# One more key tile in parts in two half groups, more sums by transfer, and spreads on ScalarE: a fused attention and local-attention kernel

## The chip, the cores and the metric

The kernel runs on one core of a Trainium2 chip. The metric is the device time of one execution, in microseconds (us). Five engines work side by side, each through its own list of instructions in order: TensorE (PE, matrix products; its weight loads are shown apart as PEld), VectorE (DVE), ScalarE (ACT), GpSimd (POOL) and SyncE (SP, which here only starts transfers). They wait for one another by semaphores. Transfers are started from SP, ACT or POOL and run on 16 DMA engines.

## What is computed

The input is x, of shape (4, 64, 64, 256): four pictures of 4096 pixels with 256 channels. Two layers follow each other. Cut to what matters:

```python
# layer 0: attention of every pixel over all 4096 of its picture
q, k, v = x @ Wq + bq, x @ Wk + bk, x @ Wv + bv        # q, k: 32 channels, v: 256
attn = softmax(einsum('bnd,bmd->bnm', q, k))
x = gamma * einsum('bnm,bmc->bnc', attn, v) + x

# layer 1: a 3x3 perception, two pointwise products, then attention over a 3x3 neighbourhood
perceived = depthwise_conv3x3(x, w_perc)               # 768 channels
hid = gelu(w_up1 @ perceived)                          # 512 channels
h = x + w_up2 @ hid                                    # 256 channels
out = h + local_attention_3x3(h, w_qkv)
```

Everything is in 32-bit floats. All biases are there, too.

## The kernel before

**Slots.** The work goes through 32 slots, 8 for each picture; a slot is a block of 512 query pixels of layer 0. While slot s does the big attention of its block, layer 1 follows behind in the same slot's instructions: the perception of block s-2, the hidden products of block s-3 and the local attention of block s-5. Everything is written out by hand in program order, and no planner moves it: what an engine does next is what the program says next for that engine.

**Points.** A slot has 16 points. At each, one half group of 256 keys (two key tiles of 128) is worked on; I number half groups n = 0 to 15. At point n the loop (L1246 on) does, in this order:

- loads on SP: for odd half groups with a tile in parts, the parts of the values of half group n+1 (load_one, "vo"); at even points the keys and values of groups ahead
- on ScalarE, the high part of the weights of half group n+1 where that is wanted (high_part, "ph", for both tiles; high_one, "oh", for one)
- energy: q times k for half group n+2 on TensorE ("e"), and the exponential of it on ScalarE ("p", three buffers)
- send: the transfer of p of half group n+1 where its denominators are summed by transfer
- the jobs of layer 1 for this point (hidden_part, local_product, update, guide, local_values, scores, local_sum, border)
- product: weights times values for half group n on TensorE, into four "acc" banks
- add_up on VectorE for half group n+1: low and gap parts ("pl", "pg", or "ol", "og" for one tile), and the sum of the denominators "den"
- so many steps of the convolution on VectorE (perceive, L666 and L672) as the list `share` gives for this point

After point 15 come partial_sums (den is transposed and reduced, twice with the local sums; "turned", "parts") and finish: a small product on TensorE that adds over partitions (dps, L551), its reciprocal on VectorE, the spread of the reciprocals to 512 columns (on_all, L538: a copy that repeats each, then a transpose), and the output of layer 0 with it (L561 on ScalarE, L567, L569, L575 on VectorE). Then the next slot's first energy and jobs.

**In parts.** A product of full 32-bit numbers takes TensorE several passes. To save passes, a weight p is cut into a high part (on ScalarE: p times 1 - 2^-13, rounded to the shorter form float32r), a low part p - high, and a "gap" high - 4096 low (both on VectorE); the values v have been cut in the same way beforehand (project_v, L334; kept in DRAM as packed_h, packed_f, packed_o). Three products of short numbers then stand for one of long ones, the gap's into acc banks of its own, and finish puts them together. Half groups 2, 4, ..., 14 have both tiles in parts (IN_PARTS), half groups 3, 5, ..., 13 the second tile alone (ONE_IN_PARTS); the first tile of these, and half groups 0, 1 and 15, go through TensorE whole. One-tile parts are made only in "full" slots: 3 to 30 without 7, 15 and 23. Slots 1, 2, 7, 15 and 23 are not full (7, 15 and 23 also project the keys and values of the next picture), nor are 0 and 31.

**Buffers.** vo, oh, ol and og share the four buffers of the tag "vs", in turn. ph, pl and pg have one buffer each. sent tiles (below) take the tag "sent" (one buffer) for odd half groups and "xc" (two buffers) for even ones; "turned" and the staged inputs also live in "xc".

**Denominators.** den must be the sum of p over all 16 half groups. VectorE adds most of it (L504). In full slots half groups 3 to 13 are instead added up by transfers that POOL starts (send, L470: the first of a parity copies p to the sent tile (L476), the others accumulate there (L478)), one chain for odd and one for even half groups; VectorE adds the two sent tiles to den at the end (L513).

Of the kernel before, what the change touches and what calls it, by code (L numbers as in the profile page):

```python
# [52 lines left out]
ONE_IN_PARTS = (3, 5, 7, 9, 11, 13)  # L53
BY_DMA = (ONE_IN_PARTS, (4, 6, 8, 10, 12))

# [5 lines left out]
def attention_then_perception_kernel(  # L61
# [37 lines left out]
    def unshifted():  # L99
# [107 lines left out]
        queries, keys, values, forms, staged = {}, {}, {}, {}, {}  # L207
# [7 lines left out]
        packed_o = tc.dram_tile([P, NSLOT, 2, C], F32, name="packed_o")  # L215
# [10 lines left out]
        def one_in_parts(s, n):  # L226
            return full(s) and n in ONE_IN_PARTS

# [69 lines left out]
        def block(s, G):  # L298
            return s - s % NBLK + G
# [24 lines left out]
        def load_one(s, n):  # L324
            forms[s, n] = tile_of([P, NB], "vs", f"vo_{s}_{n}", 4)
            nc.sync.dma_start(
                out=forms[s, n].rearrange("p (f c) -> p f c", c=C),
                in_=packed_o[:, block(s, n // 2)],
            )
# [4 lines left out]
        def project_v(s, pair, tag="m"):  # L334
            xc = staged[s]
            ps = bank(tag, f"v_{s}_{pair}")
            for i in range(2):
                for kin in range(CH):
                    nc.tensor.matmul(  # L339
                        ps[:, i * C : (i + 1) * C],  # L340
                        lhsT=xc[:, kin, bass.ts(2 * pair + i, P)], rhs=wv[:, kin, :],
                        start=(kin == 0), stop=(kin == CH - 1),
                    )
            of = ps.rearrange("p (t c) -> p t c", c=C)
            n = 2 * (s % NBLK) + pair
            split, one = n in IN_PARTS, n in ONE_IN_PARTS
            h = packed_h[:, s, bass.ts(pair, 2 * C)].rearrange("p (t c) -> p t c", c=C)
            if not split or s < NBLK or s >= NSLOT - NBLK:
                if s >= NBLK:
                    v = fresh(f"vs_{s}_{pair}")  # L350
                else:
                    if (0, s) not in values:
                        values[0, s] = tile_of([P, TPB, C], ("v", "vf")[s % 2], f"v_0_{s}", 2)
                    v = values[0, s][:, 2 * pair : 2 * pair + 2, :]
                nc.scalar.activation(v, of, AF.Identity, scale=SPLIT / (SPLIT + 1.0))  # L355
                nc.scalar.dma_start(
                    out=packed_v[:, bass.ts(2 * s + pair, 2 * C)],
                    in_=v.rearrange("p t c -> p (t c)"),
                )
                if not split:  # L360
                    tiles = slice(0, 1 if one else 2)
                    nc.gpsimd.dma_start(out=h[:, tiles], in_=v[:, tiles])
            if split:
                high = fresh(f"vh_{s}_{pair}")
                both = tile_of([P, 2, NB], "sent", f"vlg_{s}_{pair}")
                both = both.rearrange("p f (t c) -> p f t c", c=C)
                to = h, packed_f[:, s].rearrange("p f (t c) -> p f t c", c=C)
            elif one:
                high = fresh(f"vh_{s}_{pair}")[:, 0:1]
                both = fresh(f"vlg_{s}_{pair}").rearrange("p f (t c) -> p f t c", c=C)  # L370
                of = of[:, 1:2]
                to = h[:, 1:2], packed_o[:, s].rearrange("p f (t c) -> p f t c", c=C)
            else:
                return
            low, gap = both[:, 0], both[:, 1]
            nc.scalar.copy(low, of)
            nc.scalar.activation(high.bitcast(F32R), of, AF.Identity, scale=BELOW)
            nc.vector.tensor_tensor(low, low, high, ALU.subtract)
            nc.vector.scalar_tensor_tensor(gap, low, -SPLIT, high, ALU.mult, ALU.add)
            nc.vector.tensor_scalar(low, low, SPLIT, None, ALU.mult)  # L380
            for at, part in zip(to, (high, both)):
                nc.gpsimd.dma_start(out=at, in_=part)
# [11 lines left out]
        weights, highs, lows, gaps, sent = {}, {}, {}, {}, {}  # L394
# [22 lines left out]
        def high_one(s, n):  # L417
            high = tile_of([P, NB], "vs", f"oh_{s}_{n}", 4)
            p = weights[s, n // 2, n % 2]
            nc.scalar.activation(high.bitcast(F32R), p[:, 1, :], AF.Identity, scale=BELOW)  # L420
            highs[s, n] = high

        def product(s, G, half):
            p = weights[s, G, half]
            first = G == 0 and half == 0
            if first:
                n = 2 * CH if in_two_sums(s) else CH
                accs[s] = [bank("acc", f"acc_{s}_{c}") for c in range(n)]
            v = values[s, G][:, 2 * half : 2 * half + 2]
            last = G == NG - 1 and half == 1  # L430
            if not in_parts(s, G, half):
                one = one_in_parts(s, 2 * G + half)
                for i in range(1 if one else 2):
                    for c in range(CH):
                        nc.tensor.matmul(  # L435
                            accs[s][c], lhsT=v[:, i, bass.ts(c, P)], rhs=p[:, i, :],
                            start=(first and i == 0), stop=(last and i == 1),
                        )
                if one:
                    at = s, 2 * G + half  # L440
                    f = forms.pop(at)
                    for w, to, x in (
                        (v[:, 1], 0, highs[at]), (f[:, :C], 0, lows[at]), (f[:, C:], CH, gaps[at])
                    ):
                        for c in range(CH):
                            nc.tensor.matmul(  # L446
                                accs[s][to + c], lhsT=w[:, bass.ts(c, P)].bitcast(F32R),
                                rhs=x.bitcast(F32R), start=False, stop=False,
                            )
                return  # L450
            f = forms.pop((s, G, half))
            n = IN_PARTS.index(2 * G + half)
            for part, (w, to, x) in enumerate((
                (v, 0, highs[s, G, half]), (f[:, :2], 0, lows[s, G, half]), (f[:, 2:], CH, gaps[s, G, half])
            )):
                for i in range(2):
                    for c in range(CH):
                        nc.tensor.matmul(  # L458
                            accs[s][to + c], lhsT=w[:, i, bass.ts(c, P)].bitcast(F32R),
                            rhs=x[:, i, :].bitcast(F32R),  # L460
                            start=(to > 0 and n == 0 and i == 0),
                            stop=(to > 0 and n == len(IN_PARTS) - 1 and i == 1),
                        )

        def by_dma(s, n):
            if n in BY_DMA[1]:
                return full(s)
            return 0 < s < NSLOT - 1 and (s < 2 or s % NBLK < NBLK - 1) and n in BY_DMA[0]

        def send(s, n):  # L470
            p = weights[s, n // 2, n % 2]
            even = 1 - n % 2
            if n == BY_DMA[even][0]:
# [6 lines left out]
        def add_up(s, G, half):  # L480

            n = 2 * G + half
            if one_in_parts(s, n):
                low, gap = (tile_of([P, NB], "vs", f"o{x}_{s}_{n}", 4) for x in "lg")
                high = highs[s, n]
                nc.vector.tensor_tensor(
                    low.bitcast(F32R), weights[s, G, half][:, 1, :], high, ALU.subtract
                )
                nc.vector.scalar_tensor_tensor(
                    gap.bitcast(F32R), low, -SPLIT, high, ALU.mult, ALU.add  # L490
                )
                lows[s, n], gaps[s, n] = low, gap
            p = weights[s, G, half]
            if G == 0 and half == 0:
                sums[s] = tile_of([P, 2, NB], "den", f"den_{s}")
                return
            den = sums[s]
            before = weights[s, 0, 0] if (G, half) == (0, 1) else den
# [4 lines left out]
            if not by_dma(s, n):  # L503
                nc.vector.tensor_tensor(den, before, p, ALU.add)  # L504
# [5 lines left out]
            if G == NG - 1 and half == 1:  # L510
                for even in range(2):
# [26 lines left out]
        def on_all(values, turned, out):  # L538

            nc.vector.tensor_copy(  # L540
# [426 lines left out]
        def border_terms(s):  # L967


            for to, of in border_parts(s):  # L970
                nc.vector.tensor_scalar(edge[:, to], of(0), wc[:, 0:1], None, ALU.mult)
# [221 lines left out]
        for slot in range(NSLOT):  # L1193
# [29 lines left out]
            share = [1, 5, 8, 6, 5, 2, 7, 4, 6, 3, 4, 2, 1, 0, 0, 0]  # L1223
# [22 lines left out]
            for point in range(points):  # L1246
                G, half = divmod(point, 2)
                after = slot + (G + 1) // NG, (G + 1) % NG
                if one_in_parts(slot, point + 1):
                    load_one(slot, point + 1)  # L1250
# [11 lines left out]
                if one_in_parts(slot, point + 1):  # L1262
                    high_one(slot, point + 1)
                if after[0] < NSLOT:
                    energy(*after, half)
                if by_dma(slot, point + 1):
                    send(slot, point + 1)
# [534 lines left out]
```

## Time and profile before

Three runs took 3248.18 us in the median (3248.05 to 3251.35).

| | |
|---|---|
| profiled execution, its own time | 3249.86 us |
| its span | 3248.1 us |
| granted clock of TensorE | 0.999 |
| whole matmuls of the attention, L435 | 1872 instructions, 854.5 us |
| matmuls of tiles in parts, both tiles, L458 | 3 x 812, 264.0 + 223.3 + 218.7 us |
| matmuls of one tile in parts, L446 | 3 x 300, 153.9 + 94.1 + 93.3 us |
| VectorE: sums of denominators, L504 (den with p) | 161, 1287 ns each |
| VectorE: sums of denominators, L504 (p with p) | 32, 1216 ns each |
| VectorE: ol, L486, and og, L489 | 150 each, 682 and 722 ns |
| VectorE: spread, L540 | 59, 424 ns each |
| VectorE: border products, L971 | 64, 224 ns each |
| POOL: start of an accumulating transfer, L478 | 235, 857 ns each |
| sent transfers | 287 of 512 KB, 6.2 us to landing |
| vo loads | 150 of 256 KB, 4.1 us to landing |
| DMA engines over one full slot (1123.8 to 1218.3 us) | 0.71 busy |

How to read it: the profile is one execution. Busy time counts what an engine computes; a matmul of 32-bit numbers is recorded as two instructions, and matmuls overlap, so the distance from start to start tells more than a duration. Successive slots start some 94.5 us apart where they are full (dps at 1123.78, 1218.31 and 1312.75 us). In the timeline the brackets give the idle time of the engine before the line and what ended it.

### The profile page before, as it was taken

The page shows a single profiled execution, that of the slowest core. Times are in us where ns is not written, and L with a number is a line of the kernel's source. Part 1 is how long each engine was busy: PE and PEld are TensorE (multiplying, and loading weights), DVE is VectorE, ACT ScalarE, POOL GpSimd, SP SyncE. Part 2 cuts the span into 40 slices and gives each one's busy share as a digit, 9 for nine tenths or more (in the row PEclk, how much of TensorE's full clock was granted, in tenths as well). Part 3 has the DMA queues.
Part 4 walks back from the last instruction along what each step waited for, and adds up shares of the span by engine and source line. Part 5 has one row for each costly group of instructions (what it writes and reads, how often), then busy time and mean ns, then how long its engine had stood idle before and what let it go on. Part 6 is the DMA issues. An engine that isn't in the chain of part 4 may idle for free.

```text
span 3248.1 us, 37927 instructions
## 1 busy us (share of the span) xinstructions
PE 3218.2 (99%) x12286; PEld 2223.2 (68%) x12286; DVE 2866.3 (88%) x4380; ACT 1449.8 (45%) x1845; POOL 724.1 (22%) x970
## 2 busy tenths in 40 slices
PE   9999999999999999999999999999999999999998
PEld 5557767766776677676767767776677677667655
DVE  4779899898999999988999999998799999999895
ACT  4434444444444444444444444444444444444331
POOL 3201122221222221222122222211221122222021
PEclk9999999999999999999999999999999999999999
DMA  7767766777667777667766677776777666777100
GB/s 254 222 165 202 194 187 191 202 230 205 196 187 200 211 211 191 186 196 243 205 191 193 184 200 213 208 194 192 253 210 195 190 191 185 201 210 204 49 25 28
DMA packets 289964, 616.58 MB, mean 190 GB/s; under 512 B 97424, under 2 KB 98464, under 8 KB 289632
## 3 DMA queue, kind: packets, MB, share of 16 engines
q1 hardware_dynamic: 228608, 409.47, 40.5%
q0 software_dynamic: 53472, 191.17, 24.8%
q10 hardware_dynamic: 7680, 13.44, 1.1%
q8 instruction: 102, 1.67, 0.2%
q14 instruction: 102, 0.84, 0.1%
HBM read 386.24 MB, written 76.41 MB: 142 GB/s over the span
## 4 chain that ended last, share of the span: by engine, by line
PE 75%; DVE 17%; issue 3%; DMA 2%; ACT 1%; POOL 1%; SPq 0%; ACTq 0%; DVEq 0%; POOLq 0%
PE acc L435 19%; PE acc L458 11%; PE dx L836 5%; PE e L404 5%; DVE perc L666 5%; PE hid_bc L779 5%; PE hid_de L779 4%; PE hid_gf L779 4%; PE acc L446 4%; PE v L339 3%; PE lv L999 3%; PE g L932 3%; PE lo L1133 2%; PE hid_a L779 2%; DVE den L513 2%
## 5 line engine op out<-in xcount | busy, mean ns | idle before, releaser
L666 DVE SCALAR_TENSOR_TENSOR perc<-xp,wb,perc 128x526 f32<-128x526 f32 (+1 forms) x1356 | 941.2, 758 | 1.5 <-ACT perc L662 1.4
L435 PE MATMUL acc<-p,v 128*128 128x512 f32 x1872 | 854.5, 592 | 0.2 <-ACT v L355 0.2
L409 ACT ACTIVATE p<-e 128x1024 f32<-128x1024 f32 x512 | 524.3, 1024 | 546.6 <-PE e L404 490.5
L435 PEld LDWEIGHTS acc<-p,v 128*128 128x128 f32 x1872 | 351.7, 190 | 341.9 <-issue 328.2
L478 POOL DMA_DIRECT2D sent<-p x235 | 201.3, 857 | 1125.6 <-ACT p L409 948.9
L404 PE MATMUL e<-qa,ka 128*128 128x512 f32 x1024 | 368.3, 440 | 2.0 <-ACT p L409 1.1
L414 ACT ACTIVATE ph<-p 128x1024 fp32r<-128x1024 f32 x203 | 214.3, 1056 | 213.2 <-PE acc L458 131.6
L506 DVE SCALAR_TENSOR_TENSOR pg<-pl,ph 128x1024 fp32r<-128x1024 f32 x203 | 267.2, 1316 | 9.0 <-PE e L404 0.5
L502 DVE TENSOR_TENSOR pl<-p,ph 128x1024 fp32r<-128x1024 f32 x203 | 252.2, 1242 | 18.5 <-ACT ph L414 16.8
L458 PE MATMUL acc<-ph,v 128*128 128x512 f32 x812 | 264.0, 447 | 0.2 <-DMA v<-packed_h 0.2
L404 PEld LDWEIGHTS e<-qa,ka 128*128 128x128 f32 x1024 | 189.5, 189 | 88.2 <-issue 45.7
L420 ACT ACTIVATE oh<-p 128x512 fp32r<-128x512 f32 x150 | 94.5, 630 | 317.6 <-PE acc L446 265.4
L836 PE MATMUL dx<-hid,wup 128*128 128x512 f32 x512 | 229.8, 592 | 0.0
L458 PE MATMUL acc<-pl,vf 128*128 128x512 f32 x812 | 223.3, 397 | 0.0
L458 PE MATMUL acc<-pg,vf 128*128 128x512 f32 x812 | 218.7, 391 | 0.9 <-DVE pg L506 0.9
L504 DVE TENSOR_TENSOR den<-den,p 128x1024 f32<-128x1024 f32 x161 | 207.1, 1287 | 5.7 <-ACT p L409 5.3
L1088 POOL TENSOR_TENSOR lsum<-lsum,lp 128x99 f32<-128x99 f32 (+1 forms) x179 | 208.8, 1173 | 11.7
L458 PEld LDWEIGHTS acc<-ph,v 128*128 128x128 f32 x812 | 148.2, 189 | 51.3 <-issue 26.8
L458 PEld LDWEIGHTS acc<-pl,vf 128*128 128x128 f32 x812 | 152.7, 188 | 37.1
L458 PEld LDWEIGHTS acc<-pg,vf 128*128 128x128 f32 x812 | 152.5, 188 | 37.2 <-DVE pg L506 1.4
L802 ACT ACTIVATE hid<-hid,bup 128x512 f32<-128x512 f32 x120 | 80.2, 715 | 211.0 <-DVE hid L786 211.0
L672 DVE TENSOR_TENSOR perc<-perc 128x262 f32<-128x262 f32 x360 | 167.6, 486 | 6.3
(217 smaller groups left out, 4953.3 us busy)
## 6 DMA issues: line engine op xcount, KB each, us to landing
sent<-p POOLq DMA_DIRECT2D x287, 512.0 KB, 6.2
vf<-packed_f SPq DMA_DIRECT2D x203, 512.0 KB, 5.4
v<-packed_h SPq DMA_DIRECT2D x200, 512.0 KB, 4.4
ka<-packed SPq DMA_DIRECT2D x1016, 64.0 KB, 2.8
vo<-packed_o SPq DMA_DIRECT2D x150, 256.0 KB, 4.1
xp<-in_x SPq DMA_DIRECT2D x30, 528.0 KB, 6.1
packed_f<-vlg POOLq DMA_DIRECT2D x28, 512.0 KB, 4.5
xc<-in_x SPq DMA_DIRECT2D x56, 256.0 KB, 3.9
```

The costliest lines, as they stand in the source:

```text
L404: nc.tensor.matmul(e[:, i, :], lhsT=keys[s, G][:, bass.ts(2 * half + i, P)].bitcast(F32R), rhs=queries[s].bitcast(F32R), start=True, stop= ...
L409: nc.scalar.activation(p, e, AF.Exp)
L414: nc.scalar.activation(high.bitcast(F32R), weights[s, G, half], AF.Identity, scale=BELOW)
L435: nc.tensor.matmul(accs[s][c], lhsT=v[:, i, bass.ts(c, P)], rhs=p[:, i, :], start=(first and i == 0), stop=(last and i == 1),)
L458: nc.tensor.matmul(accs[s][to + c], lhsT=w[:, i, bass.ts(c, P)].bitcast(F32R), rhs=x[:, i, :].bitcast(F32R), start=(to > 0 and n == 0 and ...
L502: nc.vector.tensor_tensor(low.bitcast(F32R), p, high, ALU.subtract)
L504: nc.vector.tensor_tensor(den, before, p, ALU.add)
L506: nc.vector.scalar_tensor_tensor(gap.bitcast(F32R), low, -SPLIT, high, ALU.mult, ALU.add)
L666: nc.vector.scalar_tensor_tensor(acc, win, wt, acc, ALU.mult, ALU.add)
L779: nc.tensor.matmul(ps[:, n * C : (n + 1) * C], lhsT=w(j), rhs=rows_of(mixes[s, j][:, kind, :]), start=(j == 0), stop=(j == MULT - 1),)
L836: nc.tensor.matmul(ps, lhsT=wup2[:, d, bass.ts(c, P)], rhs=hids[s][:, d, :], start=(d == 0), stop=(d == NHC - 1),)
L1088: nc.gpsimd.tensor_tensor(to, to, near_ws[block, half][:, t_, of, :], ALU.add)
```

## The change

Five edits, in one diff:

1. ONE_IN_PARTS gains half groups 1 and 15, so these too have their second key tile in parts in full slots. project_v makes the parts of the values for them. The gap's banks now end with half group 15. (BOTH_IN_PARTS, for both tiles in this way, is empty.)
2. In full slots the denominators of half groups 0 to 13 are summed by transfer, 14 of 16 (2 to 13 in slots 8, 16 and 24, the first of a picture). The first p that VectorE adds is kept (firsts) until a second one comes, so in most full slots den is p14 + p15, and then the two sent tiles. send is called with the half group that may belong to the next slot.
3. The copy that spreads the reciprocals (on_all) is on ScalarE.
4. The first product of each border term is on ScalarE.
5. The list `share` has other numbers, with the same sum of 54: none after point 10.

```diff
-ONE_IN_PARTS = (3, 5, 7, 9, 11, 13)
-BY_DMA = (ONE_IN_PARTS, (4, 6, 8, 10, 12))
+ONE_IN_PARTS = (1, 3, 5, 7, 9, 11, 13, 15)
+BOTH_IN_PARTS = ()
+BY_DMA = (3, 5, 7, 9, 11, 13)
+BY_DMA_IF_FULL = tuple(range(14))
...
+        def alone(s, n):
+
+            return [i for i, ns in enumerate((BOTH_IN_PARTS, ONE_IN_PARTS)) if full(s) and n in ns]
...
+        def high_alone(s, n):
+            for i in alone(s, n):
+                high = rests[s, n, i][0]
+                if high is None:
+                    high = tile_of([P, NB], "vs", f"oh_{s}_{n}", 4)
+                p = weights[s, n // 2, n % 2][:, i, :]
+                nc.scalar.activation(high.bitcast(F32R), p, AF.Identity, scale=BELOW)
+                highs[s, n, i] = high
+
+        def low_and_gap(s, n):
+            for i in alone(s, n):
+                high, (_, low, gap) = highs[s, n, i], rests.pop((s, n, i))
+                if low is None:
+                    low, gap = (tile_of([P, NB], "vs", f"o{x}_{s}_{n}", 4) for x in "lg")
+                p = weights[s, n // 2, n % 2][:, i, :]
+                nc.vector.tensor_tensor(low.bitcast(F32R), p, high, ALU.subtract)
+                nc.vector.scalar_tensor_tensor(
+                    gap.bitcast(F32R), low, -SPLIT, high, ALU.mult, ALU.add
+                )
+                lows[s, n, i], gaps[s, n, i] = low, gap
...
         def by_dma(s, n):
-            if n in BY_DMA[1]:
-                return full(s)
-            return 0 < s < NSLOT - 1 and (s < 2 or s % NBLK < NBLK - 1) and n in BY_DMA[0]
+            if full(s):
+                return n in BY_DMA_IF_FULL and (n > 1 or s % NBLK > 0)
+            return 0 < s < NSLOT - 1 and (s < 2 or s % NBLK < NBLK - 1) and n in BY_DMA
...
             if not by_dma(s, n):
-                nc.vector.tensor_tensor(den, before, p, ALU.add)
+                if s in sums:
+                    nc.vector.tensor_tensor(sums[s], sums[s], p, ALU.add)
+                elif s in firsts:
+                    sums[s] = tile_of([P, 2, NB], "den", f"den_{s}")
+                    nc.vector.tensor_tensor(sums[s], firsts.pop(s), p, ALU.add)
+                else:
+                    firsts[s] = p
...
         def on_all(values, turned, out):
 
-            nc.vector.tensor_copy(
+            nc.scalar.copy(
                 squares(turned), values.unsqueeze(2).to_broadcast([P, NJ, SQ])
             )
             nc.vector.transpose(out, turned)
...
             for to, of in border_parts(s):
-                nc.vector.tensor_scalar(edge[:, to], of(0), wc[:, 0:1], None, ALU.mult)
+                nc.scalar.mul(edge[:, to], of(0), wc[:, 0:1])
                 nc.vector.scalar_tensor_tensor(
                     edge[:, to], of(1), wc[:, 1:2], edge[:, to], ALU.mult, ALU.add
                 )
...
-            share = [1, 5, 8, 6, 5, 2, 7, 4, 6, 3, 4, 2, 1, 0, 0, 0]
+            share = [2, 6, 8, 4, 7, 2, 7, 4, 6, 4, 4, 0, 0, 0, 0, 0]
...
-                if one_in_parts(slot, point + 1):
-                    load_one(slot, point + 1)
+                load_alone(slot, point + 1)
...
-                if one_in_parts(slot, point + 1):
-                    high_one(slot, point + 1)
+                high_alone(slot, point + 1)
                 if after[0] < NSLOT:
                     energy(*after, half)
-                if by_dma(slot, point + 1):
-                    send(slot, point + 1)
+                at = behind[0], 2 * behind[1] + behind[2]
+                if by_dma(*at):
+                    send(*at)
```

load_alone takes the place of load_one in the same way; add_up calls low_and_gap(s, n) where it made ol and og itself; product goes through a list of (weights, banks, values) in the same order as before.

## The prediction

> **What bounds the kernel now.** I read the page's busy table first.
>
> ```profile
> PE 3218.2 (99%) x12286; PEld 2223.2 (68%) x12286; DVE 2866.3 (88%) x4380; ACT 1449.8 (45%) x1845; POOL 724.1 (22%) x970
> ```
>
> The span is 3248.1 us, so TensorE is idle for 29.9 us in all. Work taken from any other engine can give back no more than that; time comes mainly out of TensorE work, and is lost wherever TensorE is made to wait. So I read next the timeline of one ordinary slot's end (slot 12, TensorE and ScalarE) and the chain of waits over the same stretch.
>
> ```profile
> 1201.38 0.63 PE L446 MATMUL acc<-ol,vo 128*128 128x512 f32 x2
> ...
> 1209.52 0.63 PE L446 MATMUL acc<-ol,vo 128*128 128x512 f32 x2
> ...
> 1214.46 3.59 PE L435 MATMUL acc<-p,v 128*128 128x512 f32 x8
> 1218.31 0.41 PE L551 MATMUL dps<-parts,fold 128*128 128x32 f32 x2 [0.25 <-DVE parts L533]
> ```
>
> ```profile
> 1202.10 0.63 ACT L420 ACTIVATE oh<-p 128x512 fp32r<-128x512 f32 x1 [2.20 <-PE acc L446]
> ```
>
> ```profile
> 1206.38 1.23 DVE pl L502
> ...
> 1210.37 1.40 DVE den L504
> ...
> 1211.79 1.29 DVE den L513
> ...
> 1213.11 1.50 DVE den L513
> ...
> 1215.41 0.72 DVE turned L532
> ...
> 1217.57 0.70 DVE parts L533
> ...
> 1218.31 0.41 PE dps L551 x2
> ```
>
> The reader is to see three things. TensorE closes each slot with the small product dps, in program order, and everything of the next slot is queued behind it. VectorE's closing run (add half group 15, two sums that came by transfer, fold, two transposes with reductions) ends 0.05 us before dps, and TensorE already waits 0.25 us for it: the two engines arrive together. And oh of half group 13 starts (1202.10) just after the ol matmuls of half group 11 (1201.38 + 0.63 = 2.01): four "vs" buffers, four tiles per half group, so each oh waits until TensorE has used the one two half groups back. That is no chance meeting; the list of waits has "ACT oh L420 <- PE acc L446: 265.4, 97, 5.1" (us in total, times, longest).
>
> **The change, part by part.**
>
> Matmuls. A plain half group is 8 matmul instructions, 3.43 us in the chain; one with a key tile in parts is 1.72 (x4, L435) + 1.39 (x6, L446) = 3.11. Twenty-five slots are full (3 to 30 without 7, 15, 23), two half groups each gain: 50 x 0.32 = **-16.0 us** of TensorE, on the path.
>
> VectorE's bulk. Adds by VectorE in a full slot fall from 4 to 1 (3 in slots 8, 16, 24): 69 fewer x 1.287 (L504) = -88.8. Spreads: 59 x 0.424 (L540) = -25.0. Border products: 64 x 0.224 (L971) = -14.3. New ol and og: 50 x (0.682 + 0.722) = +70.2. New parts of values in project_v: 8 x about 1.2 (L378, L379, L380 at 128x256 took 0.65, 0.43, 0.29 at 1522.68, less overlap) = +9.5. Sum -48 us of busy time, but by the idle sum above it is worth only what TensorE waits for.
>
> The end of a slot, where it counts. Half group 15 now needs oh, ol and og before its sum. Its oh takes the buffer of half group 13's, so by the row above it starts 0.09 after 13's ol matmuls end: 1209.52 + 0.63 + 0.09 = 1210.24 in slot 12's clock. ScalarE is free then (its exp of half group 15 ran at 1207.54 to 1208.56). Then: oh 0.63 -> 1210.87; hand-over 0.03, ol to the next start 0.72 -> 1211.62; og to the next start 0.61 -> 1212.23; the one sum p14 + p15, 1.14 (start to start at 1225.60) to 1.42 (at 1210.37) -> 1213.37 to 1213.65. The rest is unchanged: first L513 to dps was 1218.31 - 1211.79 = 6.52. So dps comes at 1219.88 to 1220.17. TensorE is ready 0.32 sooner than before, at 1218.06 - 0.32 = 1217.74. It waits 2.14 to 2.43, I take 2.27 (POOL's lsum, 1206.50 to 1214.91, runs beside most of it, as beside the 1.42). The dropped add of half group 14 doesn't shorten this: without it VectorE is through with pg14 at about 1208.9 and waits for oh. Nor does the new list of shares: it empties points 11 and 12, but pl14 was held by ScalarE's ph (1205.29 + 1.07), not by convolution. Queued behind: dps holds TensorE's next slot, so the full wait is lost. 25 x 2.27 = **+56.8 us**. Against it goes what the 25 slots wait at dps now: 0.99 once, 0.85, 0.74 or nearly so in six more, about 0.2 in most others, together **-9.1 us** by the timeline.
>
> Spreads on ScalarE, in finish(). Reciprocal ends 0.81 after dps starts. ScalarE then has: spread, for which the trace has no row; its nearest are 0.505 (L923, 128x384, SBUF) and 0.630 (L420, 128x512), and I take 0.6; two products with acc, which now wait behind the spread, 1.05; the new oh of half group 1, 0.63; exp, 1.03; hid_a's copy, 0.37. That ends near dps + 4.6. TensorE's lv needs the copied bank at dps + 4.67 (1222.98). A tie: 0 to 0.5 us, I take 0.05, x25 = **+1**; the upper end is 12.5. The product with the next acc banks (dps + 6.4) has 2 us of cover. The second spread, of lrden, lies behind an exp on ScalarE and ends before VectorE is wanted by hid_de (idle 2.82 there). Border products move within VectorE's own wait for dx: nothing either way; uncovered, 64 x 0.2 = 13.
>
> [...]
>
> Slots 7, 15, 23. In slot 15 the reciprocal came at 1542.51, late behind three vlg steps, and the ScalarE chain after it now reaches hid_a's copy at about 1546.6, while lv started at 1545.58: 1.0 x 3 = **+3**. The new parts of half groups 1 and 15 cost ScalarE 0.37 + 0.39 and POOL one transfer more, at points where dps had no wait: 0, bound +3.
>
> Transfers. 69 more sums of 512 KB and 50 more loads vo of 256 KB. POOL pays 69 x 0.857 = 59 us of its idle 2524. In a full slot the sums are those of half groups 0, 1, 2, issued in the slot's first 23 us, where the windows table has DMA at 0.52 and 0.29 busy. Landing is 6.2 median, 9.7 at most; the p buffer is wanted two points later, 15 us or more. The first of them waits on POOL for VectorE's L513, and what is behind it there is only the watch of parts. vo of half group 15 is issued when half group 13 leaves TensorE (1210.6), lands 4.1 later (median), and is needed at 1214.46 + 1.72 + 0.46 = 1216.6; the worst landing, 8.8, would be 2.8 late and fall inside the new wait at dps. On SP the key and value loads stand behind it by the 3 us of that wait, and are wanted two points later. Taken as 0; without the cover, some 3 us per slot.
>
> **Sum.** -16.0 - 9.1 + 56.8 + 1 + 3 = +35.7. The profiled execution has 3249.86 around a span of 3248.1; the median of the runs is 3248.18, 1.7 lower, and I add there: 3283.9, so 3284. With the low ends (53.5 for the wait, 0, 0): +28, 3277. With the high ones (60.8, 12.5, 6): +54, 3302.
>
> **The rivals.**
>
> *Faster.* The wait at dps doesn't grow: -16.0 + 4 = 3236, or 3227 if the old waits go too. It decides at 7.5 us: if oh15 to dps takes no longer than that, TensorE (1217.74 - 1210.24) never waits. For it: VectorE loses 48 us of work and the convolution is moved off the slot's end. Against it: my chain is 9.8 us long, and none of its links is convolution. Chance 0.12.
>
> *No change.* The wait grows by just what the matmuls give, 0.64 per slot, if oh15 could start about 1 us sooner than its buffer allows now: 3248 +- 6. Chance 0.06.
>
> *Slower still.* The ScalarE chain at the slot's start runs 1 us past lv, or values arrive late there, in every full slot: +25 more, 3309. For it: the tie above has no margin. Against: exp and the copy overlap their neighbours by 0.1 each. Chance 0.07.
>
> *Mine.* 0.75.
>
> **How the numbers follow.** The time is that of my case, whose own range is 3270 to 3302. The range 3252 to 3306 leaves out "faster", most of "no change" and half of "slower still", 0.12 + 0.04 + 0.035. A difference under 0.2% (6.5 us) can't be told from none here; the three chances are 0.12, 0.06, 0.82.
>
> **What would show it.** Right: dps in full slots with an idle of about 2.3 us put down to parts; oh 15 starting at once after 13's ol matmuls; TensorE's busy time some 16 us less at a longer span. Wrong: dps idle under 0.7 us; or the lost time in front of lv, hid_a or e instead. If oh 15 starts earlier than 13's ol matmuls end, my reading of the buffers falls, and with it the forecast.

## The result, and the profile after

The changed kernel takes 3286.78 us in the median (3284.07 to 3289.73, four runs) against 3248.2 us before (3248.05 to 3251.35, four runs): a ratio of 1.0117, 95% interval 1.0099 to 1.0134. It is 1.2% slower, and 3284 was forecast. The profiled execution took 3284.07 us around a span of 3282.4, which is 34.3 more than the span before; it is the shortest of the four, and by the medians the change costs 38.6. What follows explains the 34.3 of the two profiles. The first part of the page, with busy time, share of the span and instructions:

```profile
PE 3208.3 (98%) x12386; PEld 2246.2 (68%) x12386; DVE 2788.8 (85%) x4291; ACT 1538.8 (47%) x2055; POOL 738.0 (22%) x1055
```

TensorE computes 9.9 us less and is idle for 74.1 us where it was idle for 29.9. VectorE and TensorE both have less to do, and the kernel is longer. The list of waits says where (us in total, times, longest):

```profile
PE dps L565 <- DVE parts L547: 47.5, 27, 2.3
PE dps L565 <- DMA xc<-in_x: 2.0, 1, 2.0
```

So 49.5 us are lost in front of dps. The second line is the same wait under another name: in slot 6 a transfer ended at about the same moment, and VectorE's parts ended 0.06 us before dps there as in the other slots. The end of slot 12 in the timeline (start, duration, and in brackets the idle time before and what ended it), POOL, TensorE, ScalarE and VectorE together, in order of time:

```profile
1215.69 1.22 DVE L509 TENSOR_TENSOR pl<-p,ph 128x1024 fp32r<-128x1024 f32 x1 [2.20 <-ACT ph L427]
1215.72 5.42 POOL L1102 TENSOR_TENSOR lsum<-lsum,lp 128x99 f32<-128x99 f32 x6
1218.83 0.63 PE L480 MATMUL acc<-ol,vo 128*128 128x512 f32 x2
1219.55 0.63 ACT L436 ACTIVATE oh<-p 128x512 fp32r<-128x512 f32 x1 [1.67 <-PE acc L480]
1220.21 0.69 DVE L445 TENSOR_TENSOR ol<-p,oh 128x512 fp32r<-128x512 f32 x1 [1.97 <-ACT oh L436]
1220.93 0.75 DVE L446 SCALAR_TENSOR_TENSOR og<-ol,oh 128x512 fp32r<-128x512 f32 x1
1221.61 1.25 DVE L515 TENSOR_TENSOR den<-p,p 128x1024 f32<-128x1024 f32 x1
1222.90 2.49 DVE L527 TENSOR_TENSOR den<-den,sent 128x1024 f32<-128x1024 f32 x2
1226.42 0.62 PE L480 MATMUL acc<-og,vo 128*128 128x512 f32 x2
1228.30 0.69 DVE L547 TENSOR_REDUCE parts<-turned 128x16 f32<-128x512 f32 x1
1229.04 0.41 PE L565 MATMUL dps<-parts,fold 128*128 128x32 f32 x2 [2.00 <-DVE parts L547]
1232.80 0.38 ACT L806 COPY hid<-hid_a 128x256 f32<-128x256 f32 x1
1233.72 1.89 PE L1013 MATMUL lv<-wlv,h 128*128 128x256 f32 x8
```

The first PE line is the ol product of half group 13. It ends at 1218.83 + 0.63 = 1219.46, and oh of half group 15 starts 0.09 later. Meanwhile VectorE, which has made pl and pg of half group 14, stands idle for 1.97 us. Everything that closes the slot is behind ol and og in its list, so it runs without a pause from 1220.21 to 1228.99. TensorE is through with half group 15 at 1226.42 + 0.62 = 1227.04 and waits 2.00 for dps.

**What a wait costs.** From dps to dps slot 12 is 95.62 us long, and 94.53 before. Two kernels of the experiments have no recorded wait there: e9 with 93.35 and e2, with one half group less in parts, with 93.68. Between them lie 0.33 us, one half group's gain (0.32 was forecast). Going back two half groups from e9, slot 12 of the kernel before would be about 94.0 without a wait. So a recorded wait of 2.00 costs 95.62 - 93.35 = 2.27, and one of 0.25 costs 0.53: by this estimate a stall here costs some 0.27 us more from start to start than the brackets show. Why it does, no run shows.

**The whole sum, from the starts of dps.** The 24 full slots from 4 to 30 are 29.5 us longer together. Of this 5.0 is in three slots of 97.2 us in place of 95.5, in which the granted clock falls. Slots 7, 15 and 23 take 1.0 longer, slots 0 to 3 are 0.8 shorter, slot 31 is the same. What is left, 4.6, lies behind the last dps of all (117.3 us to the end of the span in place of 112.7). Together 34.3. Two of these parts, the clock and the end, were not in the forecast.

The clock first. Stretches of the windows view (start and end; length; busy time of PE, PEld, DVE, ACT and POOL, each with its instructions; granted clock; share of the DMA engines; GB/s), three around the dps of slot 4 and two around that of slot 12:

```profile
418.57:421.98 3.41, 1.41 (x8) 0.89 (x7) 2.77 (x5) 0.00 (x0) 0.25 (x1) 1.00 0.97 353
421.99:425.40 3.41, 3.41 (x9) 2.68 (x9) 2.67 (x6) 3.00 (x5) 0.25 (x1) 0.50 0.99 306
425.40:428.81 3.41, 3.41 (x18) 2.98 (x17) 3.07 (x6) 2.80 (x5) 0.67 (x2) 1.00 0.23 87
1227.53:1230.94 3.41, 1.90 (x10) 1.68 (x11) 2.19 (x5) 1.06 (x3) 0.50 (x2) 1.00 0.96 320
1230.95:1234.36 3.41, 3.41 (x17) 2.99 (x16) 3.34 (x8) 3.41 (x7) 0.00 (x0) 1.00 0.86 299
```

After the wait of 2.00 us in slot 4, TensorE is granted half of its clock for 3.41 us, and then all of it again. (1 - 0.50) x 3.41 = 1.7 us, which is what slot 5 is longer by. After the wait of 2.00 in slot 12 nothing of the kind happens: the clock is 1.00 in both stretches. What makes the difference, no run takes apart. There are four such places, behind waits of 2.00, 2.35 and 2.35 us at dps and once at the start of slot 24; the kernel before has none. (One more, at 22.6 us, lies in the start of the program, where some of the runs have one.)

The end of the span, in the same view, after and then before:

```profile
3278.00:3280.00 2.00, 0.00 (x0) 0.00 (x0) 0.00 (x0) 0.00 (x0) 0.00 (x0) 0.50 0.00 0
3280.00:3282.40 2.40, 0.00 (x0) 0.00 (x0) 0.00 (x0) 0.00 (x0) 0.00 (x0) 0.50 0.00 0
```

```profile
3246.00:3248.00 2.00, 0.00 (x0) 0.00 (x0) 0.00 (x0) 0.00 (x0) 0.00 (x0) 0.50 0.04 12
```

Before, the span ends with the last stretch that moves data. After, 4.4 us follow in which no engine computes and no transfer moves.

### The profile page after: what moved, and what is told of

It reads as the page before. It is cut to its first block, busy times and chain, and to the rows that moved or that the text cites. A ratio compares the mean times of both kernels' runs of the same rounds, so it can differ in the third digit from the quotient of the medians.

```text
span 3282.4 us, 38674 instructions
## 1 busy us (share of the span) xinstructions
PE 3208.3 (98%) x12386; PEld 2246.2 (68%) x12386; DVE 2788.8 (85%) x4291; ACT 1538.8 (47%) x2055; POOL 738.0 (22%) x1055
## 4 chain that ended last, share of the span: by engine, by line
PE 89%; DVE 7%; issue 1%; ACT 1%; DMA 1%; POOL 0%; SPq 0%; ACTq 0%; DVEq 0%; POOLq 0%
PE acc L480 42%; PE e L417 7%; PE dx L850 6%; PE hid_de L793 5%; PE hid_gf L793 5%; PE hid_bc L793 5%; PE lv L1013 3%; PE g L946 3%; PE v L347 3%; PE lo L1147 3%; PE s L1054 2%; PE hid_a L793 2%; DVE den L527 2%; DVE parts L547 1%; DVE turned L546 1%
## 5 line engine op out<-in xcount | busy, mean ns | idle before, releaser
L480 PE MATMUL acc<-p,v 128*128 128x512 f32 x1672 | 768.6, 593 | 0.2 <-ACT v L363 0.2
L499 POOL DMA_DIRECT2D sent<-p x304 | 257.8, 848 | 1482.7 <-ACT p L422 939.4
L480 PEld LDWEIGHTS acc<-p,v 128*128 128x128 f32 x1672 | 313.7, 189 | 294.1 <-issue 279.9
L417 PE MATMUL e<-qa,ka 128*128 128x512 f32 x1024 | 359.4, 432 | 4.0 <-DMA ka<-st 1.5
L436 ACT ACTIVATE oh<-p 128x512 fp32r<-128x512 f32 x200 | 126.5, 632 | 327.0 <-PE acc L480 142.9
L480 PE MATMUL acc<-oh,v 128*128 128x512 f32 x400 | 205.4, 594 | 0.0
L445 DVE TENSOR_TENSOR ol<-p,oh 128x512 fp32r<-128x512 f32 x200 | 136.9, 685 | 45.8 <-ACT oh L436 44.2
L850 PEld LDWEIGHTS dx<-hid,wup 128*128 128x128 f32 x512 | 96.7, 189 | 98.4 <-issue 93.4
```

What stands on the lines that cost most here:

```text
L417: nc.tensor.matmul(e[:, i, :], lhsT=keys[s, G][:, bass.ts(2 * half + i, P)].bitcast(F32R), rhs=queries[s].bitcast(F32R), start=True, stop= ...
L436: nc.scalar.activation(high.bitcast(F32R), p, AF.Identity, scale=BELOW)
L445: nc.vector.tensor_tensor(low.bitcast(F32R), p, high, ALU.subtract)
L480: nc.tensor.matmul(accs[s][to + c], lhsT=w[:, bass.ts(c, P)].bitcast(kind), rhs=x.bitcast(kind), start=to not in started[s], stop=last,)
L499: nc.gpsimd.dma_start(out=sent[s, even], in_=p, accum_op=ALU.add)
L850: nc.tensor.matmul(ps, lhsT=wup2[:, d, bass.ts(c, P)], rhs=hids[s][:, d, :], start=(d == 0), stop=(d == NHC - 1),)
```

## The experiments

Each is an edit of the changed kernel unless it says otherwise. The ratio is to the kernel before, run beside it. "Slot 12" is from dps to dps, with the recorded wait at its closing dps (in e5 it holds a fall of the clock, without which slots of this kind take some 96.3); "tail" is from the last dps to the end of the span.

| | median us | ratio (95%) | slot 12 (wait) | tail |
|---|---|---|---|---|
| before | 3248.2 | | 94.53 (0.25) | 112.7 |
| after | 3286.78 | 1.0117 (1.0099 to 1.0134) | 95.62 (2.00) | 117.3 |
| e1_sums_first | 3251.16 | 1.0007 (0.9997 to 1.0017) | 94.28 (0.65) | 117.4 |
| e2_no_fifteen | 3233.34 | 0.9954 (0.9937 to 0.9970) | 93.68 (0) | 117.0 |
| e3_fill_the_wait | 3283.09 | 1.0109 (1.0092 to 1.0125) | 95.62 (filled) | 117.2 |
| e4_spreads_back | 3286.97 | 1.0118 (1.0101 to 1.0135) | 95.86 (2.23) | 116.8 |
| e5_only_fifteen | 3311.04 | 1.0193 (1.0176 to 1.0210) | 97.97 (2.35) | 113.4 |
| e6_only_one | 3242.05 | 0.9978 (0.9969 to 0.9988) | 94.20 (0.24) | 113.4 |
| e7_old_sums | 3297.40 | 1.0151 (1.0134 to 1.0168) | 95.98 (2.34) | 114.2 |
| e8_own_buffers | 3256.96 | 1.0021 (1.0011 to 1.0030) | 94.44 (0.49) | 117.1 |
| e9_even_early | 3226.09 | 0.9930 (0.9917 to 0.9944) | 93.35 (0) | 116.9 |
| e10_old_shares | 3285.57 | 1.0111 (1.0096 to 1.0126) | 95.86 (2.23) | 117.3 |
| e11_eleven_both | 3238.41 | 0.9969 (0.9958 to 0.9980) | 93.41 (0) | 116.7 |
| e12_both_and_early | 3260.49 | 1.0033 (1.0021 to 1.0045) | 93.98 (0.71) | 117.2 |

My theory: TensorE waits at dps for VectorE's closing run, because this run starts only with the oh of half group 15, which waits for a buffer. Rivals: the wait comes from one of the other edits (sums by transfer, spreads, shares, half group 1), or the order on VectorE is beside the point and it simply has too much to do.

### Where the wait comes from

**e2_no_fifteen: half group 15 whole again.**

```diff
-ONE_IN_PARTS = (1, 3, 5, 7, 9, 11, 13, 15)
+ONE_IN_PARTS = (1, 3, 5, 7, 9, 11, 13)
...
-            ends = {0: n == 2 * NG - 1, CH: n == (2 * NG - 1 if full(s) else IN_PARTS[-1])}
+            ends = {0: n == 2 * NG - 1, CH: n == IN_PARTS[-1]}
```

> The changed kernel with half group 15 whole again (half group 1 stays in parts). My theory: the wait at dps goes, TensorE does 25 x 0.32 = 8 us more than in the changed kernel; 3230 to 3242, so faster than the kernel before. Rival (sums by transfer, spreads or shares cost the time): above 3270.

The list of waits of this kernel:

```profile
PE dps L565 <- DVE parts L547: 1.4, 3, 0.9
```

Of 49.5 us 1.7 are left in all (a second entry holds the rest), and the kernel is faster than before. All the other edits are still in it, so they don't make the wait without half group 15.

**e5_only_fifteen and e6_only_one: the kernel before with one new half group.** All other edits undone, ONE_IN_PARTS = (3, ..., 13, 15) in the one and (1, 3, ..., 13) in the other.

> The kernel before with one edit of the change alone: half group 15 has its second tile in parts (half group 1 whole; sums by transfer, spreads, border products and shares as before). My theory: this edit alone brings the wait at dps, 2.0 to 2.3 us in full slots: 3248 - 8 - 9 + 50 to 57, and up to 8 for the clock's dips; 3281 to 3296. Rival (the wait needs the other edits too): below 3260.

> The kernel before with half group 1 alone put in parts. My theory: 25 x 0.32 = 8 us less TensorE work and the old waits at dps, 3239 to 3243. If the waits at dps of the kernel before (9 us) are due to VectorE's bulk of work, they stay; this run against the changed kernel without half group 15 in parts (3233.3) then tells what the sums by transfer and the spreads bring: 6 to 10 us. Rival (these bring nothing): 3230 to 3236.

Half group 1 alone does what its matmuls promise: slot 12 is 0.33 shorter at the same recorded wait, which would be 25 x 0.33 = 8.3 us, and the kernel is 6.8 us faster (0.9978). Against e2, which has half group 1 in parts and all the other edits, e6 is 8.7 us slower, within the 6 to 10 expected: that is what sums by transfer, spreads, border products and shares bring together where half group 15 is whole. The waits at dps that the kernel before has, 10.0 us in e6, are nearly gone in e2. Half group 15 alone is worse than the whole change, and above the range expected. Its list of waits:

```profile
PE dps L565 <- DVE parts L547: 37.5, 18, 2.7
PE dps L565 <- DMA ka<-packed: 22.6, 10, 2.6
```

The 60.1 us of waits in 28 places, mostly of 2.27 to 2.70, lie a little above the 2.0 to 2.3 expected. What was missed is the clock: 11 slots have a stretch of half clock, some 20 us lost by the windows view where at most 8 had been allowed for. So half group 15 is enough for the wait, without any other edit.

**e1_sums_first: the order on VectorE alone.** The sums and the fold of den come ahead of ol and og. Not one instruction is added or taken away.

```diff
 add_up:
-            low_and_gap(s, n)
+            if n < 2 * NG - 1:
+                low_and_gap(s, n)
...
                 nc.vector.tensor_tensor(den[:, 0, :], den[:, 0, :], den[:, 1, :], ALU.add)
+                low_and_gap(s, n)
```

> The changed kernel, with one thing moved: for half group 15 VectorE adds the denominators first and makes ol and og after them. No work is added or removed. My theory (VectorE sits 2 us waiting for oh of half group 15, and everything up to dps is queued behind it): that idle time is now filled with the sums, the sequence from pl14 to dps takes about 2 us less, and TensorE's wait at dps falls from 2.0 us to 0.3 at most in full slots; 3286.8 falls by 25 x 1.7 to 2.0 and by the clock's dips, to 3228 to 3240. Rival (the wait comes from more transfers, spreads on ScalarE or slower VectorE work as a whole, and not from the order at the end of a slot): within 10 us of 3286.8.

It gives back 35.6 us, nearly all of the loss, and yet misses the range: it only draws level with the kernel before. Its timeline at the end of slot 12:

```profile
1206.12 1.23 DVE L510 TENSOR_TENSOR pl<-p,ph 128x1024 fp32r<-128x1024 f32 x1 [2.20 <-ACT ph L427]
1206.14 7.89 POOL L1104 TENSOR_TENSOR lsum<-lsum,lp 128x99 f32<-128x99 f32 x6
1208.59 1.59 DVE L516 TENSOR_TENSOR den<-p,p 128x1024 f32<-128x1024 f32 x1
1212.84 0.96 DVE L529 TENSOR_TENSOR den<-den 128x512 f32<-128x512 f32 x1
1218.12 0.41 PE L567 MATMUL dps<-parts,fold 128*128 128x32 f32 x2 [0.65 <-DVE parts L549]
```

The idle time in the middle is gone: VectorE has no pause between pl of half group 14 and the end. But this run takes 1218.12 - 1206.12 = 12.0 us, where the kernel before took 1218.31 - 1206.38 = 11.9 and the changed one 13.35. Part of the 1.97 us that was idle has become work that takes longer: beside POOL's lsum, which now needs 7.89 us for what took 5.42, the sum takes 1.59 in place of 1.25 and the fold 0.96 in place of 0.69. The rest of the wait, 0.6, is this run's length, and no longer the buffer.

**e8_own_buffers: the buffer alone.** oh, ol and og (and vo) of half group 15 lie in a buffer that is free there, so its oh doesn't wait for the matmuls of half group 13.

```diff
-                if i:
+                if i and n < 2 * NG - 1:
                     f, *rest = [tile_of([P, NB], "vs", f"vo_{s}_{n}", 4)] + [None] * 3
```

> The changed kernel with vo, oh, ol and og of half group 15 in a buffer of their own (the one of hid, which is free at the end of a slot) in place of the four that half group 13 uses. My theory: oh of half group 15 then starts as soon as ScalarE is free, some 1.5 us sooner, ol follows pg14 at once, and VectorE is without a break from pl14 to dps as in the run with the sums first: the wait at dps falls to 0.5 to 0.9 us and the time to 3243 to 3256. Rival (oh is late for another reason, or VectorE's work itself is too long): wait above 1.6 us, time above 3275.

The timeline at the end of slot 12 (the four tiles bear the name vo here):

```profile
1210.14 0.63 ACT L436 ACTIVATE vo<-p 128x512 fp32r<-128x512 f32 x1
1210.81 0.69 DVE L445 TENSOR_TENSOR vo<-p,vo 128x512 fp32r<-128x512 f32 x1 [0.32 <-ACT vo L436]
1211.07 0.63 PE L480 MATMUL acc<-ol,vo 128*128 128x512 f32 x2
1220.10 0.41 PE L565 MATMUL dps<-parts,fold 128*128 128x32 f32 x2 [0.49 <-DVE parts L547]
```

oh starts before half group 13's ol matmuls (third line), not after, and VectorE's idle time falls from 1.97 to 0.32. The wait at dps falls from 2.00 to 0.49. The median is 1 us above the range, with three places of lower clock. Buffer and order are two ends of one chain: either edit cuts it, and what is left in both is mainly the length of VectorE's closing run.

### What the wait costs

**e3_fill_the_wait: three products more in the wait.** They write into dps's bank, and dps overwrites them; the result doesn't need them.

```diff
-            ps = bank("m", f"dps_{s}")[:, :n]
+            ps = bank("m", f"dps_{s}")
+            for _ in range(3 if full(s) else 0):
+                nc.tensor.matmul(
+                    ps[:, : 2 * QR * QW], lhsT=fold, rhs=near.rearrange("p a q w -> p (a q w)"),
+                    start=True, stop=True,
+                )
+            ps = ps[:, :n]
```

> The changed kernel with three more products of 396 columns, of tiles that don't change, put into the bank of dps just ahead of it in full slots, and overwritten by dps: some 2 us of TensorE work where it waits 2.0 us. Theory on the granted clock (it dips to 0.65 to 0.83 for some 4 us after some of the waits, and that costs 1.6 us each): with the wait filled the clock stays at 0.999, dps comes when it did, and the time falls by 6 to 10 us, to 3277 to 3281, although TensorE does more. Rival (the dips have nothing to do with the wait): clock 0.995 to 0.997, the time the same or up to 10 us longer.

Slot 12 is as long as without them, 95.62, and so are the other ordinary slots. No slot of 97.2 is left, and behind the first 45 us the clock stays whole to the end of TensorE's work: from dps of slot 4 to dps of slot 24 this kernel takes 2030.57 us and the changed one 2036.06. That is the 5.0 of the three slots and little more. The median is 2 us above the range. The profiled execution is 3.4 us behind at the dps of slot 4 (424.99 against 421.57): 1.4 of this is slot 3, where there was only 0.45 us of wait to fill, and most of the rest a wait of 2.0 us for a load ahead of the first dps, where no product was put in. So with the wait filled and nothing else edited, none of the changed kernel's four falls to 0.50 named above is left (mean granted clock 0.998 against 0.996).

### The other edits

**e4_spreads_back, e7_old_sums, e10_old_shares** undo one edit each.

```diff
 e4:
-            nc.scalar.copy(
+            nc.vector.tensor_copy(
...
-                nc.scalar.mul(edge[:, to], of(0), wc[:, 0:1])
+                nc.vector.tensor_scalar(edge[:, to], of(0), wc[:, 0:1], None, ALU.mult)
 e7:
-BY_DMA_IF_FULL = tuple(range(14))
+BY_DMA_IF_FULL = tuple(range(3, 14))
 e10:
-            share = [2, 6, 8, 4, 7, 2, 7, 4, 6, 4, 4, 0, 0, 0, 0, 0]
+            share = [1, 5, 8, 6, 5, 2, 7, 4, 6, 3, 4, 2, 1, 0, 0, 0]
```

> The changed kernel with the spreads of reciprocals and the first border products on VectorE again. My theory: off the path, within 6 us of 3286.8; dps still waits 2.0 us in full slots. Rival (the spread on ScalarE, behind which its products and exp now stand, is what costs): 15 us or more faster.

> The changed kernel with half groups 0, 1 and 2 summed by VectorE again, as before, so 11 of 16 by transfer. My theory: these sums are off the path; the wait at dps stays 1.9 to 2.3 us and the time within 8 us of 3286.8, on the slower side if anything. Rival (the added transfers delay loads or hold POOL): 15 us or more faster.

> The changed kernel with the list of shares of the kernel before. My theory: the convolution is off the path at the slot's end (pl14 waits for ph14 in either case), so the wait at dps and the time are the same within 8 us of 3286.8. Rival (the new shares are what hurts or helps): more than 12 us away.

Spreads, border products and shares change nothing that can be told apart. 49 us of VectorE's busy time (2837.8 against 2788.8) move the median by 0.2 us, where the four times of either kernel spread over 5 to 6 us. VectorE is 85 to 86% busy in the two, and the move bought nothing, since it doesn't shorten the run that TensorE waits for (2.23 us of wait in e4, 2.00 in the changed kernel).

The sums by transfer were costed at 0 and help: without them the kernel is 10.6 us slower, just outside the range. VectorE then adds half group 14 in its idle time while POOL's lsum runs, which takes 6.42 us in place of 5.42 and reaches further into the closing run, and og and the last sum take 0.96 and 1.39 in place of 0.75 and 1.25. Slot 12 is 0.36 longer, and so are most full slots, nearly 7 us together; eight places have a lower clock in place of four, which costs about 1.7 us each.

The tail belongs to this edit, too, since e7 differs from the changed kernel in nothing else. All four kernels with the old list of sums (before, e5, e6, e7; 287 such transfers) have a tail of 112.7 to 114.2, all ten with the new one (356) one of 116.7 to 117.4. The difference lies behind the last instruction that computes: 5.1 to 6.2 us from there to the end of the span with the old list, 8.8 to 9.4 with the new one. Why is open.

### Looking for a better version

**e9_even_early: e1, and one of the two transferred sums taken in before the closing run.** The sent tile of the even half groups is complete by then, and VectorE waits for ScalarE's ph of half group 14 anyway.

```diff
+            summed = by_dma(s, n)
+            if n == 2 * NG - 2 and full(s):
+                of = sums.get(s, p)
+                summed = s not in sums
+                if summed:
+                    sums[s] = tile_of([P, 2, NB], "den", f"den_{s}")
+                nc.vector.tensor_tensor(sums[s], of, sent.pop((s, 1)), ALU.add)
...
-            if not by_dma(s, n):
+            if not summed:
```

> The changed kernel with the sums of half group 15 ahead of ol and og, as in the run with the sums first, and one more move: VectorE adds the even sent tile (its last transfer, half group 12, has landed) to p14 or den just ahead of pl14, where it sits idle for 2.2 us waiting for ph14. No work is added. That run took 12.0 us from pl14 to dps without a pause and TensorE waited 0.55 to 0.65 us for it (1.8 in slots 8, 16, 24). My theory (the closing run of VectorE after pl14 is what decides): it gets 1.2 us shorter, the wait at dps goes in all but slots 8, 16 and 24, and the time falls from 3251 by 18 to 24 us, to 3226 to 3234. Rival (VectorE's total, or the transfers, hold the rest of the time): above 3243.

Its timeline:

```profile
1194.49 1.23 DVE L513 TENSOR_TENSOR den<-p,sent 128x1024 f32<-128x1024 f32 x1
1196.76 1.23 DVE L517 TENSOR_TENSOR pl<-p,ph 128x1024 fp32r<-128x1024 f32 x1 [1.04 <-ACT ph L427]
1207.94 0.30 PE L574 MATMUL dps<-parts,fold 128*128 128x32 f32 x2
```

The sum lies in idle time of which 1.04 us is still left behind it. The closing run is 1207.94 - 1196.76 = 11.2 us, TensorE doesn't wait at this dps (it waits 0.65 in slots 8, 16 and 24 alone), and behind no dps does the clock fall. 3226.09 us is the best of all kernels here, 0.7% below the kernel before and 1.8% below the changed one. The prediction's "faster" gave 3227 with the old waits gone.

**e11_eleven_both and e12_both_and_early: both tiles of half group 11 in parts as well.** BOTH_IN_PARTS = (11,), in e11 upon e2, in e12 upon e9; e12 also skips one turn of the "vs" buffers in project_v.

> The changed kernel with half group 15 whole (3233.3 in that run) and half group 11 with both key tiles in parts, the first tile's four buffers in that of hid, free at that point. TensorE does 25 x 0.32 = 8 us less, VectorE 25 x 1.4 = 35 us more, in the middle of a slot. My theory (a tile in parts costs nothing where VectorE has room before its result is wanted, and much at the slot's end where it has none): 3224 to 3229, dps without a wait. Rival (VectorE as a whole is at its limit, so that each tile in parts costs its 1.4 us): above 3240.

> The kernel of the run with the even sums early (3226.1), with half group 11 also in parts for both key tiles. In the run that tried that alone the full slots got 0.35 us shorter each, but parts of values made for the next picture waited for buffers out of turn (stalls of 4.2 us in slot 0 and 3.4 us in slot 23); here one unused buffer is taken so that the turn of the four vs buffers stays as it was. My theory: 25 x 0.32 to 0.35 us less TensorE work and none of those two stalls: 3217 to 3222. Rival (the stalls come from the one buffer for parts of values, not from the turn): 3224 to 3232.

Both missed. In e11 the full slots gain some 0.3 us each, as expected, but two stalls of TensorE that come once take more than that: 4.2 us in slot 0 and 3.4 in slot 23, with a fall of the clock at 80.0 and 2315.8 us; the two slots are 5.6 and 5.4 us longer than in e2. The timeline around the second (POOL, ScalarE, TensorE):

```profile
2306.12 5.94 POOL L1102 TENSOR_TENSOR lsum<-lsum,lp 128x99 f32<-128x99 f32 x6
2312.60 0.60 POOL L370 DMA_DIRECT2D packed_h<-vs  x1 [0.23 <-issue]
2314.63 0.60 ACT L390 ACTIVATE vh<-v 128x512 fp32r<-128x512 f32 x1 [3.57 <-DMA packed_h<-vs]
2315.28 0.20 PE L997 MATMUL c<-edge,ones 128*1 128x16 f32 x2 [3.37 <-ACT vh L390]
```

ScalarE waits for a transfer that POOL starts only once lsum is done, and TensorE waits for ScalarE. That the turn of the buffers makes it was my guess; e12 skips one, and both stalls are still there (4.3 and 3.4). So skipping a turn doesn't help, and the cause is open. e12 has a second fault:

```profile
1116.15 1.06 ACT L428 ACTIVATE ph<-p 128x1024 fp32r<-128x1024 f32 x1 [0.48 <-PE acc L481]
1117.64 1.21 DVE L514 TENSOR_TENSOR den<-p,sent 128x1024 f32<-128x1024 f32 x1
1118.78 1.40 DVE L518 TENSOR_TENSOR pl<-p,ph 128x1024 fp32r<-128x1024 f32 x1
1129.63 0.41 PE L575 MATMUL dps<-parts,fold 128*128 128x32 f32 x2 [0.93 <-DVE parts L557]
```

ph is ready at 1117.21, but pl starts 1.6 us later, with no idle time before it: the gap in which e9 does its early sum is used up, as I read it by the parts of the second tile (no run takes them apart). The wait at dps is back.

## Why the prediction was right, point by point

**The mechanism.** The wait is at dps, VectorE's parts ends it, and oh of half group 15 starts 0.09 us after half group 13's ol matmuls, as forecast. The traces show this; e2, e8 and e1 show by taking away half group, buffer or order that it is the cause. The rival "faster" was to decide at 7.5 us from oh to dps. It is 1229.04 - 1219.55 = 9.49 us (9.8 forecast).

**Matmuls, -16.0.** Right from start to start: 0.33 us per half group in e6 and between e2 and e9. The sign named for it, some 16 us less busy time, didn't come: TensorE is busy 9.9 us less. I estimate that the four stretches of half clock add up to 4 x 1.7 = 6.8 to it.

**The wait, +56.8 - 9.1.** The step that was mis-sized. The recorded wait is mostly 1.9 to 2.0 us (48.7 in the 25 full slots), not 2.27. I took VectorE's operations as long as they were before, beside POOL's lsum; but with VectorE idle for 1.97 us beside it lsum took 5.42 us in place of 8.34, and the operations of VectorE behind it were shorter, too (1.25 us for the sum, where 1.40 stood before; 2.49 for the two sent tiles, where 2.81 stood before). On the other hand, by the estimate above, every stall costs 0.27 more than recorded, the old ones as well as the new. Without the fall of the clock the full slots are 24.5 us longer, and the forecast's terms for them come to -16.0 - 9.1 + 56.8 + 1 = 32.7: 8 too much.

**The clock, not in the sum.** +5.0 in three full slots.

**The ScalarE chain, +1.** The tie held. The spread took 0.62 (0.6 forecast), hid_a's copy ended 1232.80 + 0.38 - 1229.04 = 4.14 after dps (4.6 forecast), lv came at dps + 4.68 (4.67 in the forecast) without a wait. Over the whole span lv waits 0.9 us, in two places. "Slower still" didn't come.

**Slots 7, 15, 23, +3.** They took 1.0. Behind the dps of slot 15 lv does wait for hid_a's copy, as forecast, but for 0.47 us in place of 1.0.

**Transfers, 0.** Wrong on both sides: by e7 they make the kernel 10.6 us faster, although 3 to 4 us are lost behind the last instruction that computes. In particular "the dropped add of half group 14 doesn't shorten this" held for the order and not for what runs side by side.

**Spreads, border products and shares, 0.** Right, by e4 and e10. The sum of VectorE's busy time, -48, was off: it fell by 77.5. Steps that no edit touched became shorter too: the 360 additions of the convolution (perc<-perc) took 155.3 us together in place of 175.0. As forecast, this was worth nothing by itself.

So that the total, 35.7 for 34.3, is nearer than its terms is luck: 8 us too much in the wait and 2 in slots 7, 15 and 23 were made up for by the clock and the tail, which were not thought of.

## What to carry to other kernels

Where an engine closes a slot for another, read its closing instructions in program order and look for idle time inside them: whatever doesn't depend on the late operand belongs ahead of it. The same instructions in another order were worth 35.6 us here, and 60.7 with one sum moved further up, while taking 49 us of work off the same engine elsewhere was worth nothing as long as the wait at the slot's end stood. And a matmul saving is only had if the chain that makes its operands is no longer than the saving leaves room for: half group 1 paid, half group 15 paid only after its closing run had been put in order.

## What the runs showed of the hardware

**After some of the longer waits the granted clock fell to half.** In the changed kernel it fell to 0.50 at 421.99, 845.24, 1650.78 and 2360.76 us, each time for 3.41 us, which costs about 1.7 us by (1 - 0.50) x 3.41. The first three lie behind waits at dps of 2.00, 2.35 and 2.35 us, the fourth at the start of slot 24, where TensorE had waited 0.33 and 1.21 us. But most waits of such lengths passed without a fall, also one of 2.34 us (dps at 2457.63). e7, whose waits are 2.24 to 2.35 us, has 8 such places, and e5 (2.27 to 2.70) 11; the mean granted clock is 0.996 in the changed kernel, 0.994 in e7 and 0.993 in e5. The kernel before, whose waits at dps are 0.99 us at most, has none, and e3, in which the wait is filled, has none behind the first 45 us. What parts the waits with a fall from those without, no run takes apart.

At the end of the span, TensorE's last matmul ends at 3240.79 us before the change and 3270.85 after it, and the clock falls to 0.50 2.2 and 4.7 us later.

**Beside one another, POOL's lsum and some operations of VectorE took longer.** Six additions of lsum take 5.42 us in the changed kernel, where VectorE is idle for 1.97 of them, 6.42 in e7, 7.06 in e9, 7.89 in e1 and 8.34 before; VectorE's sum of two weights takes 1.25 behind these six and 1.59 beside them, its fold 0.69 or 0.96. Not every operation is slower beside them: pl, which starts with them, takes 1.22 or 1.23 in all of these. So e1, which moves work into the idle time beside lsum, didn't gain all of that time: its closing run took 12.0 us, where 13.35 - 1.97 = 11.4 would have been left.

**A full product and three short ones.** In the chain before, the two full products of a key tile stand as four instructions and take 1.72 us (L435 x4 at 1199.36), the six short ones of a tile in parts stand as six and take 1.39 (L446 x6 at 1201.08).
